# Layer 1's two projections as products of halves, with VectorE and ScalarE queued by hand up to the gates

## Chip, core and metric

The kernel runs on one core of one Trainium2 chip. The time is that of one execution on the device, in microseconds (us). A core has five engines that run beside each other, each with a queue of its own that it works off in order: TensorE (PE in the profile; PEld is its weight load), VectorE (DVE), ScalarE (ACT), GpSimd (POOL) and SyncE (SP, which here only issues loads and stores). An instruction that has to wait for another engine holds up everything behind it in its own queue.

## What is computed

Four graph layers on 512 nodes of 512 features, with 16384 edges. Before each layer the nodes are normalised and cut at zero, and each layer's result is added to x. Layer 0 is attention with a feed-forward part, layer 1 a projection plus a mean over neighbours, layer 2 four experts of two layers each with gates, layer 3 a convolution. The change is in layer 1, and in what stands just before and after it:

```python
    h = jnp.maximum(_layernorm(x, axis=-1), 0.0)
    x = x + _L1_gnn_ref(h, L1_gnn_wc, L1_gnn_wn, L1_gnn_bias, edge_index)
...
        alpha = x @ wc
        beta = x @ wn
        sums = jax.ops.segment_sum(beta[dst], src, num_segments=x.shape[0])
        counts = jax.ops.segment_sum(jnp.ones_like(src, dtype=beta.dtype), src, num_segments=x.shape[0])
        gamma = sums / counts[:, None]
        return alpha + gamma + bias
```

## The kernel before

Everything stays on the chip between the layers. The 512 rows lie as four blocks of 128 (NB = 4); the 512 features are four slices of 128 (KB = 4). `xs` holds x, `h` the normalised rows, `hT` the same transposed (slice of features by rows), `CT` and `C` the matrix of edge counts and its transpose. A weight is one tile of 128 x 4 x 512 (1 MB), five of them at a time; a load waits until the last reader of the tile before it is done.

Products are of two kinds. In float32 a matmul of 512 columns is two instructions in the trace; in fp32r it is one, and a value is then split into a high half (a rounded copy, made by ScalarE) and a low half (the rest, by VectorE). Layer 2 already takes its 512x512 products as seven products of halves (Strassen in Winograd's form): `left_sums` and `right_sums` (L799 to L818) form the sums of quarters on VectorE, `seven` (L820) runs the seven products into three PSUM banks, and `plus` (L832) adds what must be added on the way out.

Layer 0's feed-forward part ends with `ff_down(2)` and `ff_down(3)` (L427), each 8 steps of one block. `norm2_a`, `norm2_b` and `norm2_c` (L433 to L446) then give that block's x and its normalised `h`. The vectors made of degrees (`ideg`, `icnt`, `isd`, `nanf`) are formed after that, L719 to L732.

Layer 1, L735 to L775: `beta_of(b)` is a block's 512x512 result in four float32 matmuls of 512 columns, split into halves; `alpha_of(b)` the same for wc, added into `xs`; `gamma_of(b)` multiplies the counts with beta's halves (`psu`), scales and adds (L756), normalises (`stats_begin` L151, `norm_relu_begin` L170, `norm_relu_end` L179), writes `h` (L182) and the high half `hs` (L184), and the low half (L758). `turn` (L188) transposes a block of `h` on TensorE, and ScalarE copies it into `hT` (L194). After that come, block by block, the gates' product `pg` and the sums over neighbours `pag` (L780 to L791), then `right_sums` of `hT` and of `agT`, and layer 2's first expert (`hidden`, L882).

What sets the order: inside `tc.manual_schedule(engines=...)` the named engines keep the order of the text. Up to the end of the feed-forward part these are TensorE, VectorE and ScalarE; from layer 1 on it is TensorE alone, and a scheduler orders VectorE's and ScalarE's instructions, also across the parts. So the sums of the first two experts' weights (L802 to L806) stand on VectorE between the steps of layer 0 and layer 1, wherever the scheduler put them: four during `ff_down(2)`, the rest among beta, alpha and the first gamma.

Of the kernel before, what the change touches and what calls it, by code (L numbers as in the profile page):

```python
# [8 lines left out]
F32 = mybir.dt.float32  # L9
# [9 lines left out]
P = 128  # L19
# [17 lines left out]
def fast(  # L37
# [386 lines left out]
    def ff_up(hf, f):  # L424
        ff_up_out(hf, f, ff_up_mm(hf, f))
# [54 lines left out]
    with tc.manual_schedule(engines={ET.PE, ET.DVE, ET.Activation}):  # L480
# [204 lines left out]
        for b in (2, 3):  # L685
            affine1(b)
        nc.vector.reciprocal(ideg_b, ideg_b)
        ff_up(1, 4)
        ff_up(1, 6)
        banks[:] = [(ps_mm, "mm")]  # L690
# [6 lines left out]
        n1 = norm2_b(2, *norm2_a(2, y))  # L697
        norm2_c(2, n1)
        ff_down(3, p3, range(FB))
    y23 = residual(p3, 3, "y2")  # L700
    soft.release()
    att.release()
    ps_x.release()
# [1 line left out]
    ps_mm.release()  # L705
    ps = tc.alloc_tile_pool(name="ps", bufs=8, space=PSUM, reuse_waits="tile")
    banks[:] = [(ps, "ps")]
    norm2_c(3, norm2_b(3, *norm2_a(3, y23)))
    ffp.release()

    def split(hi, lo, full, copy):

        copy(hi, full)  # L713
        nc.vector.tensor_sub(lo, full, hi.bitcast(F32))

    main = ctx.enter_context(tc.tile_pool(name="main", bufs=1, reuse_waits="tile"))
    two = ctx.enter_context(tc.tile_pool(name="two", bufs=2, reuse_waits="tile"))

    ideg = main.tile([P, NB], F32, name="ideg")  # L719
    icnt = main.tile([P, NB], F32, name="icnt")  # L720
    nanf = main.tile([P, NB], F32, name="nanf")
    nc.vector.tensor_scalar(ideg, deg[:, :NB], 1.0, None, op0=ALU.max)
    nc.vector.reciprocal(ideg, ideg)
    isd1 = main.tile([P, NB], F32, name="isd1")
    nc.vector.tensor_scalar(isd1, deg[:, :NB], 1.0, None, op0=ALU.add)
    rs4 = rsqrt_end(*rsqrt_begin(isd1, NB, "isd"))
    isd = main.tile([P, NB], F32, name="isd")
    nc.vector.tensor_copy(isd, rs4)
    nc.vector.tensor_scalar(icnt, cnt, 1.0, None, op0=ALU.max)
    nc.vector.reciprocal(icnt, icnt)  # L730
    nc.vector.reciprocal(nanf, cnt)
    nc.vector.tensor_scalar(nanf, nanf, 0.0, None, op0=ALU.mult)  # L732


    wcs, wns = load_w(wc, "wcs"), load_w(wn, "wns")  # L735
    bias1_b = load_bc(bias1, "bias1_b")

    pair = main.tile([P, 2, NB, D], F32, tag="pair", name="pair")
    beta = pair.bitcast(R)
    hs = main.tile([P, 2, NB, D], R, tag="hs", name="hs")  # L740

    def beta_of(b):
        p = bank(f"pbe{b}")
        mm(p, [(blk(hT, k, b), wns[:, k, :]) for k in range(KB)])
        split(beta[:, 0, b, :], beta[:, 1, b, :], p, nc.scalar.copy)

    def alpha_of(b):
        nc.vector.tensor_add(xs[:, b, :], xs[:, b, :], bias1_b)
        p = bank(f"pal{b}")
        mm(p, [(blk(hT, k, b), wcs[:, k, :]) for k in range(KB)])  # L750
        nc.vector.tensor_add(xs[:, b, :], p, xs[:, b, :])

    def gamma_of(b):
        p = bank(f"psu{b}")
        mm(p, [(blk(CT, j, b), beta[:, i, j, :]) for j in range(NB) for i in range(2)])
        nc.vector.scalar_tensor_tensor(xs[:, b, :], p, icnt[:, b:b + 1], xs[:, b, :], op0=ALU.mult, op1=ALU.add)  # L756
        norm_relu((b,), "n2_", hs[:, 0, b, :])
        nc.vector.tensor_sub(hs[:, 1, b, :], h[:, b, :], hs[:, 0, b, :].bitcast(F32))  # L758

    with tc.manual_schedule(engines={ET.PE}):  # L760
        beta_of(0)
        turn(hT, h, 2, "h2_")
        beta_of(1)
        alpha_of(0)
        alpha_of(1)
        turn(hT, h, 3, "h2_")
        beta_of(2)
        beta_of(3)
        alpha_of(2)
        alpha_of(3)  # L770
        for b in range(NB - 1):
            gamma_of(b)
        turn(hT, h, 0, "h3_")
        gamma_of(3)
        turn(hT, h, 1, "h3_")  # L775

    ct_p.release()
    te_p = ctx.enter_context(tc.tile_pool(name="te_p", bufs=1, side="right", reuse_waits="tile"))
# [4 lines left out]
    with tc.manual_schedule(engines={ET.PE}):  # L783
        for b in range(NB):
# [4 lines left out]
                                     stop=(b == NB - 1 and i == 1))  # L789
            if b < 2:  # L790
                turn(hT, h, b + 2, "h3_")  # L791

    def quarter(t, a, b):
        return t[:, 2 * a:2 * a + 2, W * b:W * (b + 1)]

    def left_sums(t, s, keep=None):  # L799

        a11, a12, a21, a22 = (quarter(t, j, i) for i in range(2) for j in range(2))
        nc.vector.tensor_add(s[:, 0], a21, a22)  # L802
        nc.vector.tensor_sub(s[:, 1], s[:, 0], a11)
        last = a21 if keep is None else keep
        nc.vector.tensor_sub(last, a11, a21)
        nc.vector.tensor_sub(s[:, 2], a12, s[:, 1])  # L806
        return a11, a12, s[:, 2], a22, s[:, 0], s[:, 1], last

    def right_sums(t, s, keep=None):

        b11, b12, b21, b22 = (quarter(t, i, j) for i in range(2) for j in range(2))
        last = b12 if keep is None else keep
        nc.vector.tensor_sub(s[:, 0], b12, b11)
        nc.vector.tensor_sub(s[:, 1], b22, s[:, 0])
        nc.vector.tensor_sub(last, b22, b12)
        nc.vector.tensor_sub(s[:, 2], b21, s[:, 1])
        return b11, b21, b22, s[:, 2], s[:, 0], s[:, 1], last

    def seven(name, terms, first, result):


        pa, pb, pc = (bank(f"{name}_{i}").rearrange("p (m n) -> p m n", m=2) for i in "abc")

        def product(p, i, some, fresh=False):
            for m in range(2):
                for l, r in some:
                    for k in range(2):
                        nc.tensor.matmul(p[:, m, :], l[i][:, k, m * P:(m + 1) * P], r[i][:, k, :], start=fresh,  # L828
                                         stop=(k == 1), skip_group_check=True)
                        fresh = False  # L830

        def plus(x, p, y):  # L832
            t = uu.tile([P, 2, W], F32, tag="u", name=f"u_{name}") if y is None else y
            nc.vector.tensor_add(t, p, x)  # L834
            return t

        for t in range(len(terms)):
            for p, i in ((pa, 0), (pb, 5), (pc, 4)):
                product(p, i, terms[t:t + 1], t == 0)
        left, right = first(pa)  # L840
        u2 = plus(right, pb, None)
        product(pb, 6, terms)
        u3 = plus(right, pb, None)
        product(pa, 1, terms)
        result(1, 1, lambda y: plus(u3, pc, y))
        result(0, 0, lambda y: pa)
        product(pb, 3, terms)
        result(1, 0, lambda y: plus(left, pb, y))
        product(pc, 2, terms)
        result(0, 1, lambda y: plus(u2, pc, y))  # L850

    ws = ctx.enter_context(tc.tile_pool(name="ws", bufs=4, reuse_waits="tile"))
    uu = ctx.enter_context(tc.tile_pool(name="uu", bufs=6, reuse_waits="tile"))

    def sums_tile(name):
        return ws.tile([P, 3, 2, W], F32, tag="ws", name=f"ws_{name}")

    def copied(p):
        t = uu.tile([P, 2, W], F32, tag="u", name="u_first")
# [77 lines left out]
    def outer(e, w, gt):  # L937
        wl, wr, bl_b = w
        eT = eTs[e]
        L = left_sums(eT, scratch[:, 0:3], scratch[:, 3])  # L940

        zz = main.tile([P, 2, NB, D], R, tag="hs", name=f"zz{e}")

        def result_z(i, j, value):
            v = value(None)
            hi, lo = (zz[:, g, 2 * i:2 * i + 2, j * W:(j + 1) * W] for g in range(2))
            split(hi, lo, v, nc.scalar.copy)

        seven(f"pz{e}", [(L, wl)], copied, result_z)
        te = te_p.tile([P, NB, D], F32, tag="te", name=f"te{e}")  # L950
        if e < NX - 1:
            bias = [bl_b[:, None, j * W:(j + 1) * W].to_broadcast([P, 2, W]) for j in range(2)]

            def first_o(p):
                ts = []
                for j in range(2):
                    t = uu.tile([P, 2, W], F32, tag="u", name=f"u_b{e}_{j}")
                    nc.vector.tensor_add(t, p, bias[j])
                    ts.append(t)
                return ts  # L960

            def result_o(i, j, value):
                t = te[:, 2 * i:2 * i + 2, j * W:(j + 1) * W]
                if (i, j) == (0, 0):
                    nc.vector.tensor_add(t, value(None), bias[0])
                else:
                    value(t)

            seven(f"po{e}", [(L, wr)], first_o, result_o)
        for b in range(NB):  # L970
            if e == NX - 1:
                p = bank(f"po{e}_{b}")
                mm(p, [(blk(eT, k, b), wr[:, k, :]) for k in range(KB)])
                nc.vector.tensor_add(te[:, b, :], p, bl_b)
                if b == 2:
                    turn(hT, h, 0, "h4_")
            close(e, b, te[:, b, :], zz, gt)
            if e == NX - 1:
                norm_relu((b,), "n3_")
                if b == 2:  # L980
                    turn(hT, h, 1, "h4_")
# [27 lines left out]
            q.dma_start(out[b * P:(b + 1) * P, c], o[:, c])  # L1009

    with tc.manual_schedule(engines={ET.PE}):
        a0, a1 = weights0(0), weights0(1)
        hidden(0, a0)
        gt = gates()
        o0 = weights1(0)
# [465 lines left out]
```

## Time and profile before

| what | value |
|---|---|
| median of 3 runs | 521.88 us (521.54 to 522.24) |
| the profiled execution | 522.04 us, of it 520.4 us from the first to the last instruction |
| TensorE busy | 482.4 us (93%), mean granted clock 0.986 |
| VectorE busy | 356.5 us (68%) |
| ScalarE busy | 155.8 us (30%) |
| ff_down(2) and ff_down(3) | 194.8 to 208.6 us in the span |
| beta and alpha | 208.6 to 236.3 us |
| gamma, gates and sums over neighbours | 236.3 to 261.4 us |
| layer 2 begins | 261.4 us |

Times inside the span count from its first instruction. In the timeline a row is a group of instructions: start, length, engine, line, operation, what is written and read, count, and in brackets how long the engine had been idle before and who released it. The chain of waits follows the last instruction back to what it waited for. A matmul that is listed with 0.59 us starts 0.43 us after the one before it: they are pipelined, so starts are counted and not lengths. The granted clock is the share of TensorE's full clock that the chip allowed.

### The profile page before, as it was taken

Reading aid. Unit: us, or ns where it says so; the run is one execution under the profiler, and the core shown is the slowest. Engines: PE = TensorE matmul, PEld = TensorE weight load, DVE = VectorE, ACT = ScalarE, POOL = GpSimd, SP = SyncE. Lnnn points to the kernel's source line nnn. Section 1 sums busy time; section 2 is a strip of 40 time slices with the busy share of each in tenths; the row PEclk is TensorE's granted clock in tenths of the full one; section 3 lists DMA queues with packets and bytes.
Section 4 is the critical chain, followed back from the end, with each engine's and each line's share of the span. In section 5 each row is a group of like instructions: output and inputs, shape, how many; then the busy total and the mean of one; then the engine's idle time right before and its main releaser. Section 6 shows DMA issues by size and latency. Waiting matters only on the chain.

```text
span 520.4 us, 5638 instructions
## 1 busy us (share of the span) xinstructions
PE 482.4 (93%) x2159; PEld 358.9 (69%) x2159; DVE 356.5 (68%) x731; ACT 155.8 (30%) x316; POOL 2.8 (1%) x10
## 2 busy tenths in 40 slices
PE   2999889697999999998999999999999999999993
PEld 1798556354774584445888888888888888885552
DVE  8899999998987776928562547831687136656642
ACT  3886344341531231312402131021202121122452
POOL 2000000000000000000000000000000000000000
PEclk9999999979999999999999999999999999999998
DMA  7810201300002133422002141200322040000002
GB/s 253 296 70 1 81 1 48 115 22 0 1 21 66 55 124 119 142 73 90 0 1 91 71 151 37 102 35 20 144 81 81 1 161 1 0 1 1 0 1 85
DMA packets 18497, 34.41 MB, mean 66 GB/s; under 512 B 1528, under 2 KB 2080, under 8 KB 18464
## 3 DMA queue, kind: packets, MB, share of 16 engines
q1 hardware_dynamic: 17504, 32.47, 18.5%
q10 hardware_dynamic: 960, 1.51, 0.8%
q8 instruction: 19, 0.31, 0.3%
q14 instruction: 14, 0.11, 0.1%
HBM read 32.93 MB, written 1.05 MB: 65 GB/s over the span
## 4 chain that ended last, share of the span: by engine, by line
PE 74%; DVE 18%; ACT 3%; issue 2%; DMA 1%; ACTq 0%; DVEq 0%
PE pe_b L828 8%; PE pff L198 5%; PE pe_a L828 5%; PE pf L430 5%; PE pe_c L828 5%; PE pq L198 5%; PE pz_b L828 3%; PE po_b L828 3%; PE pqk L198 3%; PE pwo L377 3%; PE pbe L198 3%; PE ph L198 3%; PE cps L273 2%; DVE m L304 2%; PE pz_c L828 2%; PE po_a L828 2%
## 5 line engine op out<-in xcount | busy, mean ns | idle before, releaser
L834 DVE TENSOR_TENSOR u_pe<-pe_b,u_first 128x512 f32<-128x512 f32 x12 | 8.3, 692 | 55.7 <-PE pe_b L828 55.7
L198 PE MATMUL pq<-zz,C 128*128 128x512 f32 x128 | 32.7, 409 | 0.0
L271 DVE TENSOR_SCALAR ohs<-iota_h,src_f,dw_i 128x256 bf16<-128x256 f16 x104 | 28.8, 340 | 1.7 <-PE cps L273 1.6
L198 PE MATMUL pff<-hT,w 128*128 128x256 f32 x128 | 28.6, 381 | 0.7 <-issue 0.7
L198 PEld LDWEIGHTS pq<-zz,C 128*128 128x128 f32 x128 | 24.1, 189 | 6.6 <-issue 1.2
L273 PE MATMUL cps<-ohs,ohd 128*128 128x256 bf16 x104 | 19.5, 289 | 9.7 <-DVE ohs L271 9.7
L430 PE MATMUL pf<-w,ffT 128*128 128x512 f32 x64 | 28.1, 592 | 0.0
L932 ACT ACTIVATE re<-te,gt 128x512 f32<-128x512 f32 x16 | 11.6, 723 | 54.8 <-DVE te L930 54.8
L894 ACT ACTIVATE eT<-u_pe,vecs 128x256 f32<-128x256 f32 x24 | 10.9, 500 | 56.5 <-DVE u_pe L834 56.5
L198 PEld LDWEIGHTS pff<-hT,w 128*128 128x128 f32 x128 | 24.1, 190 | 5.0 <-issue 1.7
L273 PEld LDWEIGHTS <-ohd 128*128 128x128 f16 x128 | 15.7, 145 | 13.6 <-DVE ohd L266 8.0
L299 PE MATMUL psc<-qT,kT 64*128 64x256 f32 x128 | 17.8, 421 | 4.2 <-DVE s L310 4.2
L430 PEld LDWEIGHTS pf<-w,ffT 128*128 128x128 f32 x64 | 11.9, 190 | 13.9 <-issue 13.9
L304 DVE TENSOR_REDUCE m<-psc 128x256 f32<-128x2048 f32 x8 | 18.3, 2286 | 1.7 <-PE cps L273 1.2
L310 DVE TENSOR_TENSOR s<-psc,m 128x1024 f32<-128x1024 f32 x16 | 18.8, 1215 | 0.1
L713 ACT CAST zz<-u_pz 128x512 fp32r<-128x512 f32 x12 | 7.4, 618 | 37.7 <-DVE u_pz L834 37.7
L299 PEld LDWEIGHTS psc<-qT,kT 64*128 64x128 f32 x128 | 13.2, 204 | 7.8 <-issue 6.5
L348 PE MATMUL aps<-s,v 128*64 128x256 f32 x128 | 15.8, 388 | 3.0 <-DVE nt_l L145 3.0
L338 DVE TENSOR_TENSOR s<-s,r 128x2048 f32<-128x2048 f32 x8 | 18.3, 2286 | 0.1
L311 ACT ACTIVATE s<-s 128x1024 f32<-128x1024 f32 x16 | 16.8, 1054 | 3.3 <-DVE s L310 2.8
L933 DVE TENSOR_TENSOR xs<-xs,re 128x512 f32<-128x512 f32 x16 | 11.0, 690 | 9.3 <-ACT re L932 9.3
L828 PE MATMUL pe_b<-sums,wr 128*128 128x256 f32 x64 | 16.4, 379 | 0.0
(264 smaller groups left out, 1039.9 us busy)
## 6 DMA issues: line engine op xcount, KB each, us to landing
wr<-in_L_gnn_Wr_dram SPq DMA_DIRECT2D x8, 1024.0 KB
wl<-in_L_gnn_Wl_dram SPq DMA_DIRECT2D x8, 1024.0 KB
w<-in_L_gnn_W_dram SPq DMA_DIRECT2D x5, 1024.0 KB
wk<-in_L_gnn_Wk_dram SPq DMA_DIRECT2D x1, 1024.0 KB
wq<-in_L_gnn_Wq_dram ACTq DMA_DIRECT2D x1, 1024.0 KB
wv<-in_L_gnn_Wv_dram SPq DMA_DIRECT2D x1, 1024.0 KB
wo<-in_L_gnn_Wo_dram SPq DMA_DIRECT2D x1, 1024.0 KB
bl_b<-in_L_gnn_bl_dram SPq DMA_DIRECT2D x4, 256.0 KB
```

The costliest lines, as they stand in the source:

```text
L198: nc.tensor.matmul(p, a, c, start=(i == 0), stop=(i == len(pairs) - 1))
L271: nc.vector.tensor_scalar(ohs, iota_h, src_f[:, c:c + 1], dw_f[:, c:c + 1], op0=ALU.is_equal, op1=ALU.mult)
L273: nc.tensor.matmul(cps, ohd[0][:, :, c % 8], ohs, start=(c == 0), stop=(c == NCH - 1))
L299: nc.tensor.matmul(psc[i][:, 4 * g + j, :], kT[o:o + HD, j, b * P:(b + 1) * P], qT[o:o + HD, j, cols], start=True, stop=True)
L304: nc.vector.tensor_reduce(m, psc[i].rearrange("p h n -> p n h"), axis=AX.X, op=ALU.max)
L310: nc.vector.tensor_sub(s[:, g, :], psc[i][:, g, :], m[:, None, :].to_broadcast([P, 4, W]))
L311: nc.scalar.activation(s[:, g, :], s[:, g, :], AF.Exp, scale=1.0 / 8.0)
L338: nc.vector.tensor_mul(s, s, rz[i].to_broadcast([P, H, W]))
L348: nc.tensor.matmul(aps[hf][j // 2][o:o + HD, j % 2, :], v[:, b, (2 * j + g) * HD:(2 * j + g + 1) * HD], s[:, 4 * g + j, :], start=(b == 0 ...
L377: nc.tensor.matmul(p, blk(qT, k, b), wo[:, k, :], start=(k == 0), stop=(k == KB - 1))
L430: nc.tensor.matmul(p, ffT[b // 2][:, f, c:c + P], w2[f // 4][:, f % 4, :], start=(f == 0), stop=(f == FB - 1))
L828: nc.tensor.matmul(p[:, m, :], l[i][:, k, m * P:(m + 1) * P], r[i][:, k, :], start=fresh, stop=(k == 1), skip_group_check=True)
```

## The change

It does four things.

- Beta and alpha are each made of seven products of halves. `seven` isn't used for it: its steps are written out one by one, beta's and alpha's products in turn, so that a wait of one can lie beside a product of the other. `left_sums`, `right_sums` and `split` are cut into single steps for it (`left_steps`, `right_steps`, `split_hi`). The sums are formed on VectorE: four of wns, four of hT, four of wcs. Beta and alpha come out by quarters (two blocks of rows by 256 columns).
- All of layer 1 from block 3's normalisation to the gates is queued by hand on TensorE, VectorE and ScalarE. The residual of block 3 (`y23`) moves into the part before.
- The eight sums of expert 0's first two weights (`f0`) are placed among gamma's steps. What follows (gates, sums over neighbours) is still ordered by hand for TensorE alone.
- The vectors made of degrees are formed in the feed-forward part, behind `ideg_b`'s reciprocal.

The diff, cut to its core:

```diff
         nc.vector.reciprocal(ideg_b, ideg_b)
+        ideg = const.tile([P, NB], F32, name="ideg")
...
+        rs4 = rsqrt_end(*rsqrt_begin(isd1, NB, "isd"))
...
+        nc.vector.tensor_scalar(nanf, nanf, 0.0, None, op0=ALU.mult)
         ff_up(1, 4)
         ff_up(1, 6)
...
-    with tc.manual_schedule(engines={ET.PE}):
-        beta_of(0)
-        turn(hT, h, 2, "h2_")
-        beta_of(1)
-        alpha_of(0)
-        alpha_of(1)
-        turn(hT, h, 3, "h2_")
-        beta_of(2)
-        beta_of(3)
-        alpha_of(2)
-        alpha_of(3)
-        for b in range(NB - 1):
-            gamma_of(b)
-        turn(hT, h, 0, "h3_")
-        gamma_of(3)
-        turn(hT, h, 1, "h3_")
...
+    def product(p, i, some, fresh=False):
+
+        for m in range(2):
+            for l, r in some:
+                for k in range(2):
+                    nc.tensor.matmul(p[:, m, :], l[i][:, k, m * P:(m + 1) * P], r[i][:, k, :], start=fresh,
+                                     stop=(k == 1), skip_group_check=True)
+                    fresh = False
...
+    with tc.manual_schedule(engines={ET.PE, ET.DVE, ET.Activation}):
+        RB, rb = right_steps(wns, sums_tile("wns"))
+        L, ls = left_steps(hT, sums_tile("hT"))
+        RA, ra = right_steps(wcs, sums_tile("wcs"))
+        B, A = [(L, RB)], [(L, RA)]
...
+        product(ba, 0, B, True)
+        nc.scalar.copy(ub, ba)
+        a3 = norm2_a(3, y23)
+        turn(hT, h, 2, "h2_")
+        product(aa, 0, A, True)
+        nc.scalar.copy(ua, aa)
+        rb[0]()
+        n3 = norm2_b(3, *a3)
+        add_bias1(0)
+        norm2_c(3, n3)
+        rb[1]()
+        product(ba, 1, B)
+        product(aa, 1, A)
+        lo00 = beta_quarter(0, 0, ba)
+        turn(hT, h, 3, "h2_")
+        rb[2]()
+        add_bias1(1)
+        ls[0]()
...
+        product(bc_, 4, B, True)
+        ls[1]()
+        product(bb, 5, B, True)
+        ra[0]()
+        product(ac, 4, A, True)
+        ls[2]()
+        ra[1]()
+        product(ab, 5, A, True)
+        u2 = plus(ub, bb)
+        product(bb, 6, B)
+        ls[3]()
+        rb[3]()
+        ra[2]()
+        xs_plus(0, 1, ua)
+        xs_plus(0, 1, ab)
+        product(ab, 6, A)
...
+        product(ac, 2, A)
...
+        add_bias1(2)
+        add_bias1(3)
+        g = gamma_begin(0)
+        f0[0]()
+        gamma_end(0, g)
+        g = gamma_begin(1)
+        hs_low(0)
+        gamma_end(1, g)
+        f0[1]()
+        g = gamma_begin(2)
+        hs_low(1)
+        turn(hT, h, 0, "h3_")
+        gamma_end(2, g)
+        f0[2]()
+        g = gamma_begin(3)
+        hs_low(2)
+        turn(hT, h, 1, "h3_")
+        gamma_end(3, g)
+        for step in f0[3:5]:
+            step()
+        hs_low(3)
+        for step in f0[5:]:
+            step()
...
     with tc.manual_schedule(engines={ET.PE}):
-        a0, a1 = weights0(0), weights0(1)
+        a0, a1 = F0, weights0(1)
```

`gamma_begin(b)` is the first half of `gamma_of`: `psu`, the scale-and-add into `xs`, the statistics and the cut at zero. `gamma_end(b)` is the scale and the writes of `h` and `hs`, and `hs_low(b)` the low half.

## Prediction

> **What bounds the kernel now.** I read the engine shares first. The three lines give the span, and busy time (share) and instruction count of each engine.
>
> ```profile
> span 520.4 us, 5638 instructions
> ## 1 busy us (share of the span) xinstructions
> PE 482.4 (93%) x2159; PEld 358.9 (69%) x2159; DVE 356.5 (68%) x731; ACT 155.8 (30%) x316; POOL 2.8 (1%) x10
> ```
>
> TensorE (PE) works 93% of the span. A change pays if it takes work from PE without opening gaps. Second, the chain that ended last, around layer 1 (start, length, what):
>
> ```profile
> 208.56 3.43 PE pbe L198 x8
> ...
> 223.17 6.88 PE pbe L198 x16
> ...
> 259.42 1.98 PE pag L788 x8
> 261.40 1.73 PE pe_a L828 x8
> ```
>
> Beta and alpha are PE all the way: 3.43 us for a block's 512x512 result; a product of halves (pe_a) takes 1.73. Layer 2 starts at 261.40; that is the point I carry the changed kernel to. Third, the timeline, for what PE waits for and what VectorE (DVE) charges:
>
> ```profile
> 242.54 0.75 DVE L756 SCALAR_TENSOR_TENSOR xs<-psu,icnt,xs 128x512 f32<-128x512 f32 x1
> 244.11 0.72 ACT L182 ACTIVATE h<-nr_n,rs_n 128x512 f32<-128x512 f32 x1 [2.96 <-DVE rs_n L149]
> 244.88 0.66 PE L193 MATMUL tp_h<-ident,h 128*128 128x128 f32 x4 [2.38 <-ACT h L182]
> ...
> 256.54 0.69 DVE L813 TENSOR_TENSOR sums<-hT 128x512 f32<-128x512 f32 x1 [1.26 <-ACT hT L194]
> 257.15 0.68 DVE L815 TENSOR_TENSOR sums<-hT 128x512 f32<-128x512 f32 x1
> ```
>
> The only long PE wait of layer 1 is 2.38 us, for the normalised block 0 (L182). DVE takes 0.60 us from start to start of independent 128x512 sums (256.54 to 257.15), 0.72 if one reads the other. Fourth, the stages by microsecond; the figure before the DMA share is TensorE's granted clock:
>
> ```profile
> 245.00:246.00 1.00, 1.00 (x7) 0.92 (x8) 0.53 (x1) 1.00 (x4) 0.00 (x0) 1.00 0.00 0
> 246.00:247.00 1.00, 1.00 (x5) 0.82 (x4) 1.00 (x8) 0.35 (x3) 0.00 (x0) 0.68 0.00 0
> 247.00:248.00 1.00, 1.00 (x3) 0.34 (x2) 0.28 (x4) 0.76 (x2) 0.00 (x0) 0.50 0.00 0
> 248.00:249.00 1.00, 1.00 (x7) 0.98 (x6) 0.77 (x2) 1.00 (x2) 0.00 (x0) 0.50 0.00 0
> 249.00:250.00 1.00, 1.00 (x8) 1.00 (x7) 1.00 (x2) 1.00 (x3) 0.00 (x0) 0.62 0.00 0
> ```
>
> The wait is paid twice: for 3.4 us from 246.4 (0.64 + 1 + 1 + 0.76, by the shares below 1.00) the clock is halved, which costs 3.4 / 2 = **1.7 us** where PE is the bound. A wait of 1.70 left it whole:
>
> ```profile
> 66.42 2.00 PE L299 MATMUL psc<-qT,kT 64*128 64x256 f32 x16 [1.70 <-DVE s L310]
> 66.00:68.00 2.00, 1.58 (x14) 1.61 (x16) 1.93 (x5) 1.65 (x3) 0.00 (x0) 1.00 0.00 0
> 68.00:70.00 2.00, 2.00 (x8) 0.88 (x6) 2.00 (x2) 0.62 (x1) 0.00 (x0) 1.00 0.00 0
> ```
>
> **The change part by part**, in the profiled execution's clock (522.04 us: span 520.40 and 1.64 around it). The median of the runs is 521.88; I put the difference on the median.
>
> *Reciprocals into the feed-forward.* Twelve DVE operations of 4 columns, about 0.19 us each, and two on ScalarE (0.2 each): 2.3 us. DVE is idle from 192.9 to 199.05 (6.19 us behind the Wr load), so they are free; uncovered they would cost 2.3. ScalarE's logarithm now stands ahead of the evictions of pff_4 and pff_6 and waits for the 3.35 us reciprocal of ideg_b, till 193.4. So pff_4's eviction ends at 194.6 instead of 191.4 and pff_6's at 195.5; the first reader is the fifth step of ff_down(2), at 194.83 + 4 x 0.86 = 198.3. Zero.
>
> *Removed from PE.* Two projections of 8 x 3.43 = 27.5 us in all become 14 products of 1.73 = 24.2: **3.3 us less**. The order of the built program has these 14 products, each of four matmuls.
>
> *What is late next: block 3.* PE is free of ff_down(3) at 208.40. Before block 3's transposes the old order had four projections (13.7 us); the new one has four products and a transpose (4 x 1.73 + 0.44), to 215.76. From block 1's rows, residual to scale took 6.77 us (180.18 to 186.95). With the sum rb[0] put in (0.60) and L182 (0.76), from 208.60, block 3 is there at 216.73: PE waits 0.97. Then transpose to copy 0.64, copy 0.59, first sum of hT 0.69: the next product starts at 218.76, another wait of 1.55. Ten products end at 236.06; the last low half of beta comes off DVE at 236.3, so psu starts at 236.3, where it starts now (236.34). The 3.3 is eaten by 2.5 of waiting and the DVE tail.
>
> *DVE has become the second bound.* Layer 1 gets 12 sums of factors, 5 plus, 9 additions into xs. From 227.4 it has almost no idle time: bias of block 3 ends at 238.7, so the first scale-and-add of gamma starts at 238.8, as now (238.80).
>
> *Gamma.* Eight sums of Wr/Wl, now done during ff_down and beta, are threaded between the blocks; per block DVE carries 0.75 + 0.72 + 0.22 + 0.08 + 0.48 for norm, 0.60 for a factor, 0.60 for hs low, 4 x 0.19. Block 0 is ready at 243.0 (now 244.83), block 1 at 246.4 (247.96), block 2 at 250.4 (249.19), block 3 at 254.9 (253.93): early first, late at the end. PE waits 0.97 and 0.99 before the transposes of 0 and 1. Moreover ScalarE's built order has hT's copy of block 0 behind the logarithm of block 2, and the copy of block 1 behind that of block 2 and the logarithm of block 3. Behind each stands a PE instruction: pg of block 0 at 249.0 (a wait of 2.18 us), pg of block 1 at 253.9 (1.69). Layer 2 then starts at 262.7. The four last factor sums and the rest of expert 1's come after block 3 on DVE; u2 of hidden(0) is ready at 272.1 and wanted at 272.9: hidden, by 0.8.
>
> *Loads.* wr0, wl0 and wr of expert 1 wait for the same readers as now. wl of expert 1 waits for layer 1's last products, lands by about 243 (5.5 us after issue, as now) and is wanted at 268: no cost. SyncE has the same order.
>
> *Sum without the clock.* 262.7 - 261.4 = +1.3. The same walk over the old order ends 0.4 late, since PE passes from alpha to psu 0.4 us faster than its terms; in the new order DVE holds that place. I take +1.1 (0.9 to 1.3).
>
> *The clock* is the unknown. Two places ask: around 215.8 to 218.8 (2.5 us of waiting, only 0.44 of transposes inside), and 245.3 to 248.9 (3.2 of 3.6 idle). The rows bound each between nothing (1.70 idle) and 1.7 us (2.38 idle). The second is past the row that fell; I give it 1.7. The first is near it, but split: I leave it at nothing and keep 1.7 for the range.
>
> [...]
>
> **Rivals.** The bound between change and none is 0.2% (1.04 us), about what a measurement of this kernel can tell.
> - A: waits as walked, clock halved once, in gamma: 521.88 + 1.1 + 1.7 = **524.7**. 0.40.
> - B: it falls before the first sums of hT too: 524.7 + 1.7 = 526.4. For it: that quiet stretch is as long as the one that fell. 0.24.
> - C: never: 521.9 + 1.1 = 523.0. For it: every single wait but one is under 1.7, and the old fall is already in the old time. 0.12, half of it within 0.2%.
> - D, faster: the two held copies cost nothing, because PE reaches pg later or ScalarE's logarithms come sooner than walked. Place: hT's copies of blocks 0 and 1. Walked with the copies right behind their transposes, layer 2 starts 2.27 us sooner, and the 3.6 us stretch shrinks to 2.1, so the clock stays: 521.9 + 1.1 - 2.3 = 520.7. It decides once over 2.1 of the 8.4 us of walked waits (0.97 + 1.55 + 0.97 + 0.99 + 2.18 + 1.69) fall away with no fall of the clock. Against it: the order on ScalarE is fixed in the build. 0.24, of it 0.20 faster by over 0.2%.
>
> That the change does not do what it says I exclude for PE's work (the order shows it); for the time, A to C say it.
>
> **How the numbers follow.** Forecast A, 524.7. The range takes in D and B with 0.5 beyond B for a second fall that overlaps the wait at pg of block 1: 520.6 to 526.9. Faster 0.20 (D); same 0.10 (half of C, the rest of D); slower 0.70.
>
> **What would show it.** Right: PE waits near 1 and 1.5 us before the transposes of block 3 and the first product of hT's sums; no long DVE idle time from 227 to 254; PE waits at pg named after ScalarE's hT copies; a clock near 0.5 around 249 to 252. Wrong: block 3 ready before 215.8; pg of block 0 following its transposes within 1 us; a layer 2 that starts before 260.4; DVE's sums well under 0.60 apart, or far more wait between engines than the old trace's 0.03 to 0.05 us.

## The result and the profile after

The changed kernel takes **527.83 us** (median of four runs, 526.54 to 528.74) against 521.77 for the kernel before in the same session: ratio 1.0113, 95% interval 1.0091 to 1.0136. It is slower by 6.1 us. The forecast was 2.8 us slower, and its range ended at 526.9.

The head of the page of the changed kernel, with span, busy time and instruction count of each engine:

```profile
span 525.9 us, 5762 instructions
PE 485.0 (92%) x2207; PEld 371.4 (71%) x2207; DVE 372.8 (71%) x753; ACT 157.4 (30%) x318; POOL 2.8 (1%) x10
```

TensorE is busy for 2.6 us longer than before, although 3.3 us of its work were taken out: something made the same instructions slower. The chain that ended last shows which (start, length, engine, what was written, line, count):

```profile
218.86 3.47 PE pbe_c L783 x8
222.33 1.94 PE pbe_b L783 x8
224.27 1.73 PE pal_c L783 x8
...
250.89 1.87 PE pg L198 x8
252.76 3.62 PE pag L947 x8
258.56 1.06 PE pg L198 x8
259.61 3.02 PE pag L947 x8
...
267.14 1.97 PE pag L947 x8
269.10 1.73 PE pe_a L783 x8
```

The first product with sums of hT takes 3.47 us, where two lines further another of the same size takes 1.73; the first two `pag` take 3.62 and 3.02, the last 1.97. Layer 2 starts at 269.10, 7.7 us later than before (261.40). The granted clock is the third figure from the end of these rows, one for each window of 3.41 us, the time for which it was halved from 219.22 on (span, PE, PEld, DVE, ACT, POOL busy, clock, DMA share, GB/s):

```profile
215.81:219.22 3.41, 1.21 (x7) 0.75 (x7) 3.04 (x6) 1.78 (x3) 0.00 (x0) 1.00 0.00 0
219.22:222.63 3.41, 3.41 (x10) 2.67 (x9) 2.12 (x4) 0.00 (x0) 0.00 (x0) 0.50 0.00 0
246.53:249.94 3.41, 1.50 (x8) 0.78 (x6) 3.20 (x11) 1.35 (x3) 0.00 (x0) 1.00 0.00 0
249.94:253.35 3.41, 2.46 (x10) 2.37 (x11) 3.27 (x9) 2.20 (x5) 0.00 (x0) 0.50 0.00 0
253.35:256.77 3.42, 3.42 (x11) 2.64 (x10) 1.50 (x5) 0.00 (x0) 0.00 (x0) 0.50 0.00 0
256.77:260.18 3.41, 1.92 (x14) 1.60 (x13) 2.01 (x7) 2.70 (x6) 0.00 (x0) 1.00 0.00 0
260.18:263.59 3.41, 3.41 (x13) 2.73 (x12) 2.83 (x5) 0.07 (x1) 0.00 (x0) 0.50 0.02 5
```

Four windows at half clock in three places, where the forecast had one; each place is called a fall of the clock below. Each of the three follows a window in which PE did little (1.21, 1.50 and 1.92 us of work). What left PE idle there is in the timeline of gamma (PE and ScalarE):

```profile
248.30 0.66 PE L193 MATMUL tp_h<-ident,h 128*128 128x128 f32 x4 [0.93 <-ACT h L182]
249.93 0.20 ACT L138 ACTIVATE lv_n<-ve_n 128x1 f32<-128x1 f32 x1 [1.06 <-DVE ve_n L161]
250.16 0.20 ACT L140 ACTIVATE r_n<-lv_n 128x1 f32<-128x1 f32 x1
250.27 0.57 ACT L194 COPY hT<-tp_h 128x512 f32<-128x512 f32 x1
250.89 1.87 PE L198 MATMUL pg<-gw,hT 128*128 128x4 f32 x8 [1.93 <-ACT hT L194]
```

The copy of hT's block 0 could have run after block 0's transposes, at 245.5; it stands behind block 2's logarithm (L138) in ScalarE's queue, runs at 250.27, and PE waits 1.93 us for it. Block 1's copy stands behind block 2's copy and block 3's logarithm:

```profile
257.11 0.59 ACT L194 COPY hT<-tp_h 128x512 f32<-128x512 f32 x1 [4.20 <-PE tp_h L193]
257.59 0.21 ACT L138 ACTIVATE lv_n<-ve_n 128x1 f32<-128x1 f32 x1
257.94 0.57 ACT L194 COPY hT<-tp_h 128x512 f32<-128x512 f32 x1
258.06 0.16 DVE L145 TENSOR_TENSOR nt_n<-r_n 128x1 f32<-128x1 f32 x1 [3.14 <-ACT r_n L140]
258.56 1.06 PE L198 MATMUL pg<-gw,hT 128*128 128x4 f32 x8 [1.49 <-ACT hT L194]
```

The first of these copies is block 2's, and it waits for transposes that stand on PE behind block 0's `pag`. So PE waits 1.49 us for what its own transposes hold up, by way of ScalarE's queue. VectorE waits 3.14 us for block 3's logarithm in that queue, while the `pag` on PE takes 3.62 us at half clock; the last one takes 1.97 at the whole clock.

The theory after this: the waits are about what the walk said, but they halve the clock three times instead of once, and that is most of the loss. Rivals: the waits alone make the time longer; the factor sums put into gamma on VectorE do; the products of halves do.

### The profile page after: what moved, and what is told of

It is laid out like the page before. It is cut to its first block, busy times and chain, and to the rows that moved or that the text cites. A ratio compares the mean times of both kernels' runs of the same rounds, so it can differ in the third digit from the quotient of the medians.

```text
span 525.9 us, 5762 instructions
## 1 busy us (share of the span) xinstructions
PE 485.0 (92%) x2207; PEld 371.4 (71%) x2207; DVE 372.8 (71%) x753; ACT 157.4 (30%) x318; POOL 2.8 (1%) x10
## 3 DMA queue, kind: packets, MB, share of 16 engines
HBM read 32.93 MB, written 1.05 MB: 65 GB/s over the span
## 4 chain that ended last, share of the span: by engine, by line
PE 72%; DVE 20%; ACT 3%; DMA 2%; issue 2%; SPq 0%; ACTq 0%; DVEq 0%
PE pe_b L783 8%; PE pff L198 5%; PE pe_a L783 5%; PE pf L430 5%; PE pe_c L783 5%; PE pq L198 5%; PE pz_b L783 3%; PE po_b L783 3%; PE pqk L198 3%; PE pwo L377 3%; PE ph L198 3%; PE cps L273 2%; DVE m L304 2%; PE pag L947 2%; PE pz_c L783 2%; PE pz_a L783 2%
## 5 line engine op out<-in xcount | busy, mean ns | idle before, releaser
L789 DVE TENSOR_TENSOR u_sum<-pe_b,u_first 128x512 f32<-128x512 f32 x12 | 8.3, 692 | 50.8 <-PE pe_b L783 50.8
L988 ACT ACTIVATE eT<-u_sum,vecs 128x256 f32<-128x256 f32 x24 | 10.9, 500 | 52.7 <-DVE u_sum L789 52.7
L726 ACT CAST zz<-u_sum 128x512 fp32r<-128x512 f32 x12 | 7.4, 618 | 37.7 <-DVE u_sum L789 37.7
L789 DVE TENSOR_TENSOR u_sum<-pz_b,u_first 128x512 f32<-128x512 f32 x12 | 8.3, 690 | 11.8 <-PE pz_b L783 11.6
```

## The experiments

Each time stands beside runs of the kernel before on the same chip; the ratio is to those.

**1. Copies of hT placed by hand.** `turn` is cut in two, and ScalarE is ordered by hand for the gates as well:

```diff
-        turn(hT, h, 0, "h3_")
+        tp = turn_mm(h, 0, "h3_")
+        pu.append(gamma_mm(3))
+        g = gamma_begin(1, pu[1])
+        turn_out(hT, 0, tp)
...
-    with tc.manual_schedule(engines={ET.PE}):
+    with tc.manual_schedule(engines={ET.PE, ET.Activation}):
```

> Only the place of two ScalarE instructions is changed: the copies of hT's blocks 0 and 1 stand right behind the exponentials of blocks 1 and 2, not behind the logarithms of the blocks after. Held-copies theory (waits as walked, and clock falls that the waits cause): the 1.93 and 1.49 us waits of PE at pg go, the walk brings layer 2 forward by 2.3 us, and with the quiet stretch of gamma cut the second and third fall of the clock (about 3 and 1.6 us in the trace) go wholly or in part: 4 to 7 us less than the changed kernel, 521 to 524 us. Waits-alone theory: 2.3 us less, 525.5. Sums-in-gamma theory (VectorE with the threaded factor sums sets gamma): under 1 us less, 527 or more.

Measured: 521.53 us, ratio 0.9993 (0.9984 to 1.0003). Two instructions of ScalarE in another place give back 6.3 us. In its timeline the copy ends before PE has need of it:

```profile
245.08 0.20 ACT L140 ACTIVATE r_n<-lv_n 128x1 f32<-128x1 f32 x1
245.19 0.57 ACT L196 COPY hT<-tp_h 128x512 f32<-128x512 f32 x1
...
247.26 0.66 PE L192 MATMUL tp_h<-ident,h 128*128 128x128 f32 x4 [0.92 <-ACT h L182]
...
247.75 0.95 PE L203 MATMUL pg<-gw,hT 128*128 128x4 f32 x8
```

`pg` follows the transposes without a wait and takes 0.95 us, not 1.87; no window of layer 1 is at half clock in the profiled execution, the fastest of the ten. From the end of `ff_down(3)` to layer 2 it is 52.2 us against 60.4. The held copies were the place; how much of it is waiting and how much the clock, this run does not tell.

**2. Factor sums out of gamma.** The first three steps of `f0` follow `hs_low(3)` with the rest.

> Only the place of three VectorE instructions is changed: the first three factor sums of expert 0, which stood between the blocks of gamma, come after the low half of block 3 with the other five. Sums-in-gamma theory: each took 0.60 us out of VectorE's chain from block to block, so layer 2 starts some 1.8 us earlier and the clock recovers: 3 us or more less than the changed kernel, 525 or below. Held-copies theory: blocks are ready 0.6 to 1.8 us earlier, but the copies are still queued behind the logarithms of blocks 2 and 3, so the waits at pg stay near 1.5 to 2 us and the falls of the clock stay: 0.5 to 2 us less, 526 to 527.3, and the factors of expert 0 come later, which may give some of it back.

Measured: 525.33 us, ratio 1.0088 (1.0061 to 1.0115): 2.5 us less, between the two theories by the time. The trace decides: PE's waits at `pg` are still there (1.32 and 1.25 us, for hT's copy), and one of the three falls of the clock is missing, the one after block 1's `pg`. The sums had a part, since they held the blocks up by 0.6 us each; the larger part of the loss stayed with the copies. How large each part is stays open: three of the five executions took 525.1 to 525.3 us, at mean clocks of 0.980 to 0.983, the other two 527.4 and 528.5 us at 0.977 and 0.974, as slow as the changed kernel.

**3. The first two waits filled.** Three products whose results nobody reads keep PE busy around block 3's transposes; the code adds `fill(flat, 1)` before and `fill(flat, 2)` behind `turn(hT, h, 3, "h2_")`.

> Three extra TensorE products of 128x256 whose results nobody reads (0.43 us each) fill the two waits ahead of the first product of hT's sums: one before the transposes of block 3, two behind them. Nothing else moves. Clock theory: the clock does not fall at 219, which gives back 1.7 us: 526.1. Waits-alone theory (the clock is not what makes the time longer): no change or up to 0.3 us more, 527.8 to 528.1. The gamma stage should look as in the changed kernel.

Measured: 526.03 us, ratio 1.0081 (1.0063 to 1.0099). PE got more work and the time fell by 1.8 us: there is no fall at 219, and the windows from 217.93 to 224.75 have the whole clock. Waits alone would not shorten the time. But this trace alone doesn't show that the filling did it: experiment 1 left the same waits unfilled, its windows lie at the same times (both have one that begins at 204.27), and its clock stayed whole here too. Experiments 4 and 7 settle it. Their windows lie 0.1 us apart, and PE's work lies alike in them; 4 has the filling and 7 has not. First 4, then 7:

```profile
216.84:220.25 3.41, 2.51 (x13) 1.64 (x12) 3.06 (x6) 1.73 (x3) 0.00 (x0) 1.00 0.00 0
220.25:223.67 3.42, 3.42 (x18) 3.01 (x17) 2.14 (x5) 0.00 (x0) 0.00 (x0) 1.00 0.00 0
```

```profile
216.95:220.36 3.41, 1.32 (x7) 1.03 (x8) 3.06 (x6) 1.70 (x3) 0.00 (x0) 1.00 0.00 0
220.36:223.77 3.41, 3.41 (x10) 2.70 (x9) 1.81 (x4) 0.00 (x0) 0.00 (x0) 0.50 0.00 0
```

Gamma did not stay quite as it was: in experiment 3 it has three windows at half clock in a row (252.1 to 262.3) instead of two and one.

**4. Gamma's waits filled too, first try.** Three products ahead of each of the two transposes, six and four ahead of `pg`.

> The three extra products of the run before, and in gamma 16 more products whose results nobody reads (128x512, 0.21 us each): three ahead of each of the transposes of blocks 0 and 1 of h, six ahead of pg of block 0 and four ahead of pg of block 1. All waits stay, PE is only kept busy in them. Clock theory: all three falls go, 1.7 + 3 + 1.6 = 6.3 us less than the changed kernel, 521.5; between 521 and 523 if one fall stays in part. Waits-alone theory: no change, 527.8.

Measured: 524.81 us, ratio 1.0049 (1.0033 to 1.0066): a miss against 521.5. The products ahead of `pg` have 256 columns, where 512 were meant, and took 0.13 us each, not 0.21; three of the six ran ahead of block 1's transposes, so 1.57 and 1.01 us of the two waits stayed, and with them two falls (251.0 and 257.8).

**5. All waits filled.** 14 and 11 products of 0.13 us, placed inside the hand-ordered part:

```diff
         turn(hT, h, 1, "h3_", 3)
+        pg = bank("pg")
+        fill_g(pg, 14)
...
                 turn(hT, h, b + 2, "h3_")
+            if b == 0:
+                fill_g(pg, 11)
```

> The changed kernel with extra products, whose results nobody reads, in every wait of layer 1: the three of 0.43 us around the transposes of block 3, three of 0.21 ahead of each transpose of h's blocks 0 and 1, and now 14 of 0.13 us directly behind the transposes of block 1 (ahead of pg of block 0) and 11 behind those of block 2 (ahead of pg of block 1), which cover the 1.93 and 1.49 us. All instructions of the changed kernel keep their order, so the waits for data stay. Clock theory: no fall in layer 1, layer 2 starts about 6.3 us earlier (1.7 + 3 + 1.6) than in the changed kernel: 521.5 us, 520.8 to 522.5. Waits-alone theory: no change, 527.8. If a fall stays in spite of the filling (as in the run before, whose filling ended 1.6 us early), the small products of pg count as idle, and the time is about 524.

Measured: 522.21 us, ratio 1.0006 (0.9997 to 1.0015). The windows in gamma, same columns as above:

```profile
245.67:249.08 3.41, 3.19 (x21) 2.54 (x20) 3.20 (x11) 1.34 (x2) 0.00 (x0) 1.00 0.00 0
249.08:252.49 3.41, 3.15 (x22) 2.68 (x21) 3.27 (x9) 2.22 (x5) 0.00 (x0) 1.00 0.00 0
```

`pg` of block 0 starts 40.7 us after `ff_down(3)`, in the changed kernel 42.4, of which 1.7 are the first fall: the data come no earlier, PE was only not idle. So the clock alone is worth 527.83 - 522.21 = **5.6 us** of the 6.1 (1.07% of 522 by the two ratios, the same). That settles it against the waits-alone theory.

**6. One part alone: the reciprocals.** The kernel before with only the operations on degrees moved.

> One part of the change alone: the kernel before, with only the twelve small VectorE operations and two ScalarE operations on the degrees moved into the feed-forward, as in the changed kernel. Prediction's step: free, no PE delay; in layer 1 of the kernel before they stood beside PE work too. Theory: no difference from the kernel before, within 0.1% (521.6 to 522.6). Rival: they cost part of their 2.3 us in the feed-forward, where ScalarE's logarithm waits for a 3.35 us reciprocal ahead of two evictions: 523 or more.

Measured: 521.70 us, ratio 0.9999 (0.9989 to 1.0008). Free, as forecast. Its trace shows something else. PE waits 2.39 us for block 0, as in the kernel before (2.38), and the clock stays; first the two windows of the kernel before, then those of this one:

```profile
242.95:246.36 3.41, 1.48 (x9) 1.30 (x10) 2.71 (x11) 2.25 (x7) 0.00 (x0) 1.00 0.00 0
246.36:249.77 3.41, 3.41 (x14) 2.65 (x12) 2.45 (x12) 2.53 (x5) 0.00 (x0) 0.50 0.00 0
```

```profile
244.21:247.62 3.41, 1.82 (x10) 1.61 (x11) 2.71 (x13) 2.25 (x7) 0.00 (x0) 1.00 0.00 0
247.62:251.03 3.41, 2.79 (x19) 2.17 (x19) 3.18 (x13) 2.88 (x5) 0.00 (x0) 1.00 0.00 0
```

The wait lies otherwise to the windows: 1.82 us of PE work fall into the one here, 1.48 there. And without the fall layer 1 is only 0.8 us shorter (52.0 against 52.8 us), not 1.7: in the kernel before, behind the fall, PE has no wait at block 1's transposes, while in this one it waits 0.62 us there. Experiments 13 to 15, with this layer as in the kernel before and no fall in it, have 52.0 to 52.1 us, and 17, with the fall, 52.8. In the time it is smaller still: of the 92 executions of the kernel before that stand beside the experiments, the 53 with a mean clock of 0.990 or more took 521.83 us on average, the other 39 took 522.04. The runs don't show which of them had this fall.

**7. Copies placed and factor sums late.**

> The copies of hT right behind the transposes, as before, and besides the three factor sums of expert 0 out of gamma, behind the low half of block 3. With the copies in place the blocks of h set the pace of gamma, 4.04 us from block to block, of which 0.60 is the factor sum. Theory: the pace becomes 3.44, layer 2 starts 1.5 to 1.9 us earlier than with the copies alone: 519.6 to 520.1 us. Rival: the factor sums of expert 0 are then late for its first products, and the gain is given back in waits at pe_b: 521.5.

Measured: 520.75 us, ratio 0.9975 (0.9965 to 0.9985), 0.8 less than the copies alone. The pace of the blocks is 3.44 us as expected, but the profiled execution has a fall at 220.4, behind the same waits of 0.8 and 1.4 us at block 3 that left the clock whole in experiment 1, and PE waits 0.44 us at `pe_b`. Both sides had a part.

**8. Plain projections, gamma by hand.** Beta and alpha as eight products of 3.43 us, the sums of expert 0 during them, copies in place.

> Layer 1's projections as eight plain products of 3.43 us again, in the order of the kernel before; reciprocals in the feed-forward, factor sums of expert 0 done during the projections, gamma queued by hand on three engines with the copies of hT in place. Tells what the products of halves bring by themselves. Theory: they bring nearly nothing, since 2.2 of their 3.3 us went into the waits for block 3 and the rest into VectorE's tail: layer 2 starts within 0.5 us of the kernel with copies and factor sums moved, 519.3 to 520.5 us. Rival: the products of halves are worth their 3.3 us once gamma is in order: this kernel at 522 or more, 2 or more behind that one.

Measured: 519.81 us, ratio 0.9966 (0.9954 to 0.9978). Without the products of halves the kernel is 0.9 us ahead of experiment 7, which has them, and by layer 1 alone 1.6 us (50.7 against 52.3). In that order they brought nothing.

**9. Beta by products of halves, alpha plain.** Alpha's blocks 0 and 1 cover the wait for block 3, block 2 the first sums of hT.

> Beta by seven products of halves, alpha by four plain products, whose blocks 0 and 1 stand ahead of block 3's transposes, block 2 behind them (over the first sums of hT) and block 3 last (over the low halves of beta). Gamma as in the two before. PE has 26.7 us of work from the end of the feed-forward to the first psu, and no wait in it: psu starts about 1.1 us earlier than in the kernel before. VectorE has nine operations less than in the changed kernel and is ahead of PE at gamma. Theory: layer 2 starts at about 257.5 on the old trace's scale (now 261.4): 518 us, 517 to 519. Rival: gamma's chain on VectorE, 3.44 us for a block, sets the end whatever psu does: 519.5 to 520.

Measured: 519.35 us, ratio 0.9955 (0.9942 to 0.9968), short of 518. PE waits twice 0.78 us for `u_sum`: the next product adds into the bank that VectorE has still to read.

**10. The same with those two products apart.**

```diff
-        product(bc_, 4, B, True)
         product(bb, 5, B, True)
         u2 = plus(ub, bb)
+        product(bc_, 4, B, True)
         product(bb, 6, B)
         u3 = plus(ub, bb)
+        half_proj(p3, 3, wcs, 0)
...
+        half_proj(p3, 3, wcs, 1)
```

> The version with beta by seven products and alpha plain, with another order of its products: the second product into bank b has the first product into bank c ahead of it, and the plain product of block 3 is cut into two halves of 1.7 us, one ahead of the next product of bank c, one at the end. In the run before, PE waited 0.78 us twice there for VectorE to read the bank that the next product adds to. Theory: both waits go, psu and with it layer 2 start 1.6 us earlier than in that run: 517.8 us, 517.2 to 518.5. Rival: low halves of beta are late instead, and psu waits for them: 519.3.

Measured: 518.75 us, ratio 0.9938 (0.9925 to 0.9952). The waits are gone and `psu` starts 2.0 us earlier, but layer 2 only 1.25: PE then waits 1.05 us for block 0, since VectorE sets the pace of gamma.

**11 and 12. Gates and sums over neighbours one place forward.** `pg` of block 0 and its `pag` no longer wait for block 1's transposes to come first; in experiment 11 on top of 10, in 12 on top of the plain projections of 8.

> As the run before it, and the gate and aggregate products of gamma moved one place forward on PE, so that only block 3's own products and block 2's aggregate follow block 3's transposes. VectorE's pace of 3.44 us a block sets gamma; the tail behind block 3 shrinks from 6.0 to 5.1 us. Theory: 0.9 us less than the run before it: 516.9 us, 516.3 to 517.8. Rival: PE's waits come to lie in one 3.41 us window and halve the clock: 518.5 or more.

> Plain projections with the same forward order of gamma as the run before it. Tells what seven products of halves for beta bring once nothing waits: by PE's work 1.7 us. Theory: 0.5 to 0.9 us less than plain projections with the former order of gamma (519.8), so 519 us, 518.4 to 519.5, and 1.5 to 2 us behind the run before it. Rival: VectorE's chain of gamma, not PE, sets the start of layer 2, and both end within 0.5 us of each other.

Measured: 517.16 us, ratio 0.9916 (0.9902 to 0.9929), and 518.77 us, ratio 0.9948 (0.9934 to 0.9962). The first is the best kernel of this study, 4.5 us ahead of the kernel before. But the difference of 1.6 us between the two isn't what it seemed: from `ff_down(3)` to layer 2 they take 49.5 and 49.8 us. The rest lies behind the last operation. In all profiles so far with plain projections the span ends 6.0 to 6.5 us after VectorE's last operation, in all with products of halves 4.3 to 4.9. That also hid 1.6 us or more of the changed kernel's loss: its last product is 7.7 us late, its time only 6.1.

**13 to 15. What the end of the span hangs on.** The kernel before, with instructions added whose results nobody reads: 24 small products, 13 settings of one column on VectorE, or both and one copy on ScalarE.

```diff
+        for _ in range(13):
+            nc.vector.memset(spare1[:, 0:1], 1.0)
```

> The kernel before with 24 products of 128x4 on the identity, whose results nobody reads, at the start, where PE waits 6.8 us for VectorE anyway. Question: in the four profiles of kernels with eight plain projections (2159 PE instructions) 6.0 to 6.5 us lie between the last VectorE operation and the end of the span, in the seven with products of halves (2183 or more) 4.3 to 4.9. If the length of PE's program decides it, this kernel's tail is 4.3 to 4.9, and its time 1.5 us less than that of the kernel before, 520.2; if not, tail 6.0 to 6.5, time 521.7.

> The kernel before with 13 settings of one column on VectorE, whose results nobody reads, in the feed-forward's 6 us in which VectorE waits for a weight. If the length of VectorE's program (731 operations against 744 or more) decides the tail: 4.3 to 4.9 us and 1.5 us less time, 520.2; if not, 6.0 to 6.5 and 521.7.

> The kernel before with both additions and one copy of a column on ScalarE: 2183 PE, 744 VectorE and 317 ScalarE instructions, as in the kernels with beta by products of halves. If the lengths of the programs decide the tail, alone or together: 4.3 to 4.9 us and 1.5 us less time, 520.2. If the tail stays at 6.0 to 6.5, it is something else that the kernels with plain projections have in common.

Measured: 523.73 us, ratio 1.0036 (1.0025 to 1.0048); **520.28 us, ratio 0.9971 (0.9960 to 0.9982)**; 522.42 us, ratio 1.0012 (1.0001 to 1.0022). The ends of the span behind VectorE's last operation: 6.1, 4.3 and 4.9 us. The 24 products were no small thing: in the trace they are 48 instructions and take 10.4 us, and the first real product starts at 13.62 us instead of 6.81, which explains what 13 and 15 lose. With VectorE's 731 operations (13) the end stays at 6.1 us, with 744 (14 and 15) it is 4.3 and 4.9. The last rows of the timeline, first of the kernel before (span 520.4), then of the one with 13 settings:

```profile
513.08 0.79 DVE L1007 TENSOR_TENSOR o<-rm,xs 128x256 f32<-128x256 f32 x2 [0.95 <-ACT rm L1006]
513.90 0.37 ACTq L1009 DMA_DIRECT2D out_dram<-o  x1
```

```profile
513.34 0.79 DVE L1010 TENSOR_TENSOR o<-rm,xs 128x256 f32<-128x256 f32 x2 [0.96 <-ACT rm L1009]
514.16 0.37 ACTq L1012 DMA_DIRECT2D out_dram<-o  x1
```

```profile
span 518.5 us, 5651 instructions
PE 482.1 (93%) x2159; PEld 358.1 (69%) x2159; DVE 357.1 (69%) x744; ACT 155.7 (30%) x316; POOL 2.8 (1%) x10
```

The last store is issued 0.26 us later, and the span ends 1.9 us earlier.

**16 and 17. The same in the plain kernel of 12, and with five settings only.**

> Plain projections with the forward order of gamma, and the 13 settings of one column on VectorE, whose results nobody reads, in the feed-forward. If the length of VectorE's program decides the tail in this kernel too, its tail goes from 6.0 to about 4.6 us and its time from 518.8 to 517.3 us: level with beta by products of halves (517.2), and then the products of halves bring nothing at all in layer 1. If the tail belongs to something else, 518.8.

> The kernel before with 5 of these settings instead of 13: 736 VectorE operations. Between 731 (tail 6.0 to 6.5) and 744 (4.4 to 4.9). If the tail falls step by step with the length, about 5.5 us and 521.2; if it has one edge, either 521.8 or 520.3.

Measured: 517.73 us, ratio 0.9922 (0.9908 to 0.9937), end of the span 4.5 us; and 520.90 us, ratio 0.9983 (0.9973 to 0.9992), end 4.85 us. With the ends alike, plain projections stand level with products of halves (0.9922 against 0.9916, the intervals overlap). Five settings already shorten the end to the lower group: 731 operations have the long end, 736 and more the short one. Why is open. In the profiles the loads of instructions (queue q14) near the end come at other moments: in the last 4 us of the span the kernel before has one, between 517.90 and 518.40, and the one with 13 settings has three, two between 515.50 and 516.50 and one in the last 0.5 us. Nothing was tried on it.

## Why the prediction was wrong

The sign and the mechanism held. The step that failed is **the clock**: "The first is near it, but split: I leave it at nothing", and for gamma "I give it 1.7". Measured, the clock is worth 5.6 us (experiment 5), not 1.7: 1.7 of it at the first place, which stood at nothing, and so some 3.9 in gamma, which stood at 1.7.

Point by point:

- *Reciprocals: zero.* Right (experiment 6).
- *3.3 us less on PE.* Right as work; the fourteen products are in the trace at 1.73 us when the clock is whole.
- *Block 3: waits of 0.97 and 1.55 us.* Measured 0.80 and 1.40; transposes at 216.80 (forecast 216.73), next product at 218.86 (218.76).
- *`psu` at 236.3, first scale-and-add at 238.8.* Measured 237.73 and 240.54. The difference, 1.4 and 1.7 us, is the first fall, which I had left at nothing. It was a coin's toss that the row with 1.70 us of idle time could not decide: the waits were alike in experiments 1 and 7, and it fell in one only.
- *Gamma: waits of 0.97 and 0.99, then 2.18 and 1.69 at `pg`.* Measured 0.97, 0.93, 1.93 and 1.49. The held copies were the right place. Blocks 0 to 2 were ready 1.8 to 1.9 us after their forecast, about the first fall, but block 3 at 259.55 and not 254.9: the walk had no term for a copy that waits for slowed transposes and holds up block 3's logarithm behind it.
- *Waits in all +1.1.* Experiment 5, with no fall, has 54.5 us from `ff_down(3)` to layer 2 against 52.8 before: +1.6. Nearly right as it was reckoned. But the 52.8 has a fall in it; against the 52.0 of experiment 6, which has none, the waits are worth 2.4.
- *One fall in gamma, 1.7 us.* Two windows in a row at 250 to 256.8, and one more at 260.2. The price of 1.7 came from the fall of the kernel before, where layer 1 loses only 0.8 by it (experiment 6). I had priced a fall as an event that belongs to one long wait. Gamma has four waits in 15 us, and three of its windows were at half clock. The first of them, from 249.94, held 1.87 us of `pg`, with its four columns, and 0.59 us of a `pag`, and the clock stayed down for the next; by then block 1's `pg` came so late that its wait of 1.49 us lay in the window from 256.77, and the third fall followed.
- *The end of the program* was in no term. It gave back about 1.6 us (experiment 14's size).

Together 1.6 + 5.6 - 1.6 = 5.6, against 6.1 measured; the rest is within the interval.

Of the rivals, B (both places fall, 526.4) had the right idea and 3.4 of the 5.6 us. D, "walked with the copies right behind their transposes", was worth 4.0 us against A in my sum, 2.3 of waits and 1.7 of the clock; on the chip it was 6.3, since it takes gamma's falls of the clock with it. The range left 0.5 us for a second fall in gamma; by the four waits there it should have left one or two more of 1.7.

## What to carry to other kernels

When TensorE is the bound, price a group of waits by windows and not by the longest wait: lay windows of 3.41 us, the length of a fall here, over the walk, and count a possible fall for each that is less than half full of work, wherever the windows may begin; here ten windows with at most 1.50 us of work led to one, and none with 1.54 us or more did. Walk the queues of the other engines too: with VectorE nearly full in gamma (busy for 3.20 and 3.27 of 3.41 us from 246.53 on), two copies in another place in ScalarE's queue were worth 6.3 us here, and 3.3 us less matrix work brought nothing. Compare two kernels up to the last operation and behind it separately, or an accident at the end is taken for a gain.

## What the runs showed of the hardware

**The falls of the clock begin whole multiples of 3.41 us apart.** So it is in the six profiles for which the start of more than one fall ahead of the last products was read (the kernel before, the changed kernel, experiments 2, 3, 4 and 7): 103.17, 219.22, 249.94 and 260.18 in the changed kernel are 34, 9 and 3 windows apart; 102.99 and 246.36 in the kernel before are 42; 104.31 and 220.36 in experiment 7 are 34. A fall lasted one window (219.22 in the changed kernel), two (249.94) or three (experiment 3, from 252.06).

**How little work led to a fall.** Counting PE's busy time in a window at full clock, without the products of four columns, ten windows of layer 1 with at most 1.50 us led to a fall, and none with 1.54 us or more did (1.54 in experiments 2 and 7, 1.82 in 6). This is without experiment 5, whose filling writes the same bank as the products of four columns, and without 16 and 17. So, as an estimate from these windows alone, the edge in layer 1 lies at 44 to 45% of a window. A wait of 2.38 us led to a fall in the kernel before, where 1.48 us of work lay in the window from 242.95, and one of 2.39 us led to none in experiment 6, where 1.82 us lay in the window from 244.21: the two executions differ in where the windows lie. In layer 0 the windows with the least work at full clock that led to no fall have 1.75 us (the kernel before, from 123.47) and 1.83 us (the changed kernel, from 123.65); 0.22 us (from 99.58) and 0.06 us (from 99.76) led to one. Leaving out the products of four columns is a choice made from these runs: with them counted, a window with 2.40 us led to a fall (experiment 4, from 254.39) and one with 1.78 did not (experiment 3, from 245.23). The transposes are counted: this last window holds 0.65 us of them and 1.13 us of other work, and the next, with 1.14 us of work and no transposes, led to a fall.

**The end of the span behind VectorE's last operation was shorter where VectorE had more operations.** With 731 operations the span ended 6.0 to 6.5 us behind the last one (five profiles); with 736 to 753, 4.3 to 4.9 (fourteen). Five settings of one column made the kernel before 1.1 us faster, thirteen 1.6 us.
